# Layer 0's down projection by seven block products a chunk instead of two full products

## The chip, the cores and the metric

The kernel runs on one core of one Trainium2 chip. The metric is the device time of one execution, in microseconds (us). All data is 32-bit floating point.

## The reference, cut to what matters

The reference is a small two-layer network. Each layer normalizes its input and adds an attention part and a feed-forward part to it. The change lies in layer 0's feed-forward part, for 2,048 tokens of width 512 and an inner width of 1,408:

```
xn  = layernorm(x)
g   = (xn @ gate_w.T) * gate_s          # 512 -> 1408
u   = (xn @ up_w.T) * up_s              # 512 -> 1408
out = ((silu(g) * u) @ down_w.T) * down_s   # 1408 -> 512: "the way down"
x   = x + attention0(xn) + out
```

Layer 0's attention is a recurrence: 32 minibatches of 16 tokens (of each of 4 sequences) follow each other, and each one updates a small state matrix that the next one needs. Layer 1, an attention with softmax and a feed-forward part of four experts, comes after layer 0 and is not touched.

## The kernel before, in words

Layer 0 works on 8 chunks of 256 tokens (4 sequences x 64 positions). TensorE (PE) multiplies 128x128 stationary blocks with moving operands of up to 512 columns and adds up in PSUM.

**Fill work.** For each chunk the generator `between(ch)` yields pieces of PE work in order. First come 11 steps `gate_up(ch, i)`: each fetches two weight tiles of 256 KB (`wg`, `wu`, two buffers each) on SP's DMA queue (L471), makes 8 products of 256 columns, and leaves 128 of the 1,408 inner rows in `hid` (L478, on DVE, after an activation on ACT). In chunk 0 `finish_constants` follows (spread of the output scale `dsc` to all partitions, the bias row `brow`). Then `down(ch, u)` runs for the two halves u of the chunk's tokens, mixed with the next chunk's keys, values and queries (`nxt`) and with the end of the previous chunk (`fin`). `down` makes 11 products of 512 columns with tiles `wd` of 256 KB, which SP fetches for each u anew into four buffers (L489). Then DVE multiplies the PSUM result by `dsc` (L494), and GpSimd (POOL) adds `brow` to the rows of x (L495) and that to the result (L496).

**The recurrence.** The main loop takes the 32 minibatches: `prepare(n)` on POOL (load of `kv`, L307, and the tiles `sk`, `km` and the queries in `wq_bd`), `weights_out`, `first_product` (the PE group `pz`), `queries_out` (the PE group `pso`), `gradient` (about 17 DVE instructions), `out_operands` (`gh` on POOL, L421), `update` (PE group `wacc`) and `emit_out`. Between these steps it calls `fill(us)`, which takes pieces from the fill work until their stated costs (the numbers that the pieces yield) cover the given time. The next minibatch's first product needs the state `wacc` that this one has updated.

**Order.** Each engine works through its instructions in the built order, and so does SP with the DMAs it issues: one that waits holds those behind it. A scheduler in the tile framework may place instructions otherwise than the program does; `tc.keep_in_program_order` pins one. A tile of a pool waits for the readers of the tile that had its buffer before.

**Early constants.** At the start POOL's queue fetches small tiles (`sel8`, `tok8`, `ch8`, the row `dsc`) into the pool `one`, whose tiles live through the whole of layer 0.

Of the kernel before, what the change touches and what calls it, by code (L numbers as in the profile page):

```python
# [18 lines left out]
P = 128  # L19
# [13 lines left out]
NS = 8  # L33
# [22 lines left out]
def trunk_kernel(ctx: ExitStack, tc: tile.TileContext, a: dict, out: bass.AP):  # L56
# [49 lines left out]
    with ExitStack() as px:  # L106
# [9 lines left out]
        def mm(out, lhsT, rhs, start=True, stop=True):  # L116
            nc.tensor.matmul(out, lhsT=lhsT, rhs=rhs, start=start, stop=stop, skip_group_check=True)  # L117
# [64 lines left out]
        nc.scalar.dma_start(out=rows_small[:, P:], in_=a["tok"].unsqueeze(0))  # L182
        bones = load(one, "bones", [P, P], eng=nc.scalar)
        m2 = load(one, "m2", [P, 2], eng=nc.scalar)
        gamma_row = wk.tile([P, HS], F32, tag="xr", name="gamma_row")
        gbeta_row = one.tile([P, HS], F32, tag="gbeta_row", name="gbeta_row")
        lrw = load(one, "lrw", [P, NC, P], a["lrw"].rearrange("(c p) m -> p c m", p=P))
        wq_w = load(one, "wq", [P, NC, HS], a["wq"].rearrange("(c p) o -> p c o", p=P))
# [12 lines left out]
        tok = lrb[:, P:]  # L201


        sel8 = one.tile([NS, P], F32, tag="sel8", name="sel8")
        tok8 = one.tile([NS, 2, 4, HD], F32, tag="tok8", name="tok8")
        for h in range(2):
            r = slice(4 * h, 4 * h + 4)
            nc.gpsimd.dma_start(
# [249 lines left out]

        gs = load(one, "gs", [P, NI], eng=nc.gpsimd)
        us = load(one, "us", [P, NI], eng=nc.gpsimd)  # L460
        dsc = one.tile([P, HS], F32, tag="dsc", name="dsc")
        nc.gpsimd.dma_start(out=row["dsc"], in_=a["dsc"].unsqueeze(0))
        hid, yf = {}, {}

# [15 lines left out]
            )  # L480
            yield 3.43

        def down(ch, u):
            xr = wk.tile([P, HS], F32, tag="xr", name=f"xr_{ch}_{u}")
            load_rows(xr, a["x"], ch, u)
            pd = ps_dn.tile([P, HS], F32, tag="pd", name=f"pd_{ch}_{u}")
            for i in range(NI):
                w = wk.tile([P, HS], F32, tag="wd", name=f"wd_{ch}_{u}_{i}", bufs=4)
                nc.sync.dma_start(out=w, in_=a["wd"][i * P : (i + 1) * P, :])  # L489
                mm(pd, hid[ch][:, i, u * P : (u + 1) * P], w, i == 0, i == NI - 1)  # L490
                if i in (3, 7):
                    yield 3.43
            t = wk.tile([P, HS], F32, tag="yf", name=f"yf_{ch}_{u}", bufs=4)
            nc.vector.tensor_mul(t, pd, dsc)  # L494
            nc.gpsimd.tensor_add(xr, xr, brow)  # L495
            nc.gpsimd.tensor_add(t, t, xr)  # L496
            yf[ch, u] = t
            yield 2.57


        ch8 = one.tile([NS, 4, 32], F32, tag="ch8", name="ch8")
        for j, name in enumerate(("gamma", "beta")):
            nc.gpsimd.dma_start(
                out=ch8[4 * j : 4 * j + 4], in_=by_head(name).rearrange("al be h d -> be al (h d)")
# [9 lines left out]

        def finish_constants():
            nc.sync.dma_start(out=wo, in_=a["wo"].rearrange("(c p) o -> p c o", p=P))
            spread_row(dsc, row["dsc"])
            pt = psum()[:, :NS]
            nc.tensor.transpose(pt, ch8.rearrange("s al x -> s (al x)"), ident[:NS, :NS])
            nc.vector.tensor_copy(by_ch, pt)  # L520
            yield 1.0

            pt = psum()[:, :NC]
            mm(pt, onesd, beta_ch)
            beta_m = wk.tile([P, 1], F32, tag="beta_m", name="beta_m", bufs=1)
            nc.vector.tensor_reduce(beta_m, pt, AX.X, ALU.add)
            nc.vector.tensor_scalar(beta_ch, beta_ch, beta_m, None, ALU.subtract)

            pr = psum()
            for c in range(NC):  # L530
                pnb_b = wk.tile([P, P], F32, tag="pnb_b", name=f"pnb_b{c}")
                nc.vector.tensor_copy(pnb_b, pnb[:, c : c + 1].to_broadcast([P, P]))
                mm(pr, pnb_b, wo[:, c, :], c == 0, c == NC - 1)
            nc.vector.tensor_copy(brow, pr)
            for c in range(NC):
                nc.vector.tensor_scalar_mul(wo[:, c, :], wo[:, c, :], pnw[:, c : c + 1])
            yield 3.43
# [118 lines left out]
        def between(ch):  # L656

            fin = finish(ch - 1) if ch > 0 else iter(())
            if ch + 1 == NCHUNK:
                latent_operands()  # L660
            for i in range(NI):
                yield from gate_up(ch, i)
                if ch + 1 == NCHUNK and i in (2, 5, 8):
                    latent_rows(i // 3)
                if i == NI - 3:
                    yield from take(fin, 1)
            if ch == 0:
                yield from finish_constants()
            nxt = iter(())
            if ch + 1 < NCHUNK:  # L670
                nxt = chain(
                    norm_turn(ch + 1), keys(ch + 1), token_tile(ch + 1, 0), token_tile(ch + 1, 1), queries(ch + 1)
                )
            else:
                yield from fin
            for u in range(2):
                dn = down(ch, u)
                for j in range(3):
                    yield from take(nxt, 2)
                    yield from take(dn, 1)  # L680
                    yield from take(fin, 1)
            yield from nxt
            done.add(ch + 1)
            yield from fin
            if ch + 2 < NCHUNK:
                norm_rows(ch + 2)
            if ch + 1 == NCHUNK:
                for key in sorted(parts, key=str):
                    yield from latents(key)
# [842 lines left out]
```

## Time and profile before

| | |
|---|---|
| median of 3 runs | 2003.97 us (2002.03 to 2005.3) |
| the profiled execution's own time | 2001.78 us |
| its span, first to last instruction | 2000.0 us |
| granted TensorE clock, mean | 0.995 |
| PE, DVE, ACT, POOL busy, share of the span | 97%, 59%, 41%, 26% |
| layer 0's end in the trace | near 970 us |
| down products (`pd`, L117) | 166.3 us busy, 352 records of 592 to 697 ns |
| DMA | 273.50 MB, 137 GB/s on average |

The profile comes from one execution. PE's busy time holds the pipelined ends of products, so the pitch from one group's start to the next group's start is the better price of a product. Idle time of an engine that nobody waits for costs nothing.

### The profile page before, as it was taken

What the parts mean: (1) busy time and instruction counts of PE and PEld (TensorE: products, weight loads), DVE (VectorE), ACT (ScalarE), POOL (GpSimd) and SP (SyncE); (2) the same over time, 40 slices, a digit from 0 to 9 for tenths busy, and PEclk for the clock granted to TensorE, in tenths of its full rate; (3) what the DMA queues carried; (4) which work ended last, traced back from release to release, by engine and by line L of the source; (5) the groups of instructions that cost most, each with busy time, mean ns of one, the idle gap of its engine ahead of it and who ended that gap; (6) DMA issues with size and microseconds to landing.
All of it is one profiled execution on the core that took longest, in us unless ns stands there. A gap on an engine that the chain in (4) does not pass through costs nothing.

```text
span 2000.0 us, 32373 instructions
## 1 busy us (share of the span) xinstructions
PE 1939.4 (97%) x11626; PEld 1233.0 (62%) x11626; DVE 1170.9 (59%) x2579; ACT 815.8 (41%) x1695; POOL 515.9 (26%) x619
## 2 busy tenths in 40 slices
PE   8999999999999999998999999999999999999997
PEld 6777676767767676743777745555555555555555
DVE  5445757475666566574555566555655556555664
ACT  2224334334334342432222165554554455445552
POOL 4334343424243343412000101111211121322110
PEclk9999999999999999999999999999999999999999
DMA  6657566646465455746652144444444434333343
GB/s 167 199 138 212 143 188 169 181 115 192 123 172 167 124 175 152 229 117 200 224 167 63 44 112 127 123 102 109 105 103 107 106 102 112 93 97 97 102 107 103
DMA packets 227307, 273.50 MB, mean 137 GB/s; under 512 B 88587, under 2 KB 117452, under 8 KB 226508
## 3 DMA queue, kind: packets, MB, share of 16 engines
q1 hardware_dynamic: 206656, 239.28, 43.5%
q0 software_dynamic: 8992, 26.84, 4.7%
q10 hardware_dynamic: 11500, 5.32, 0.9%
q8 instruction: 93, 1.52, 0.3%
q14 instruction: 66, 0.54, 0.1%
HBM read 174.18 MB, written 34.87 MB: 105 GB/s over the span
## 4 chain that ended last, share of the span: by engine, by line
PE 49%; DVE 1%; DMA 1%; SPq 0%; ACT 0%; issue 0%; DVEq 0%; ACTq 0%
PE pc L1254 11%; PE sc L1207 9%; PE pq L1184 8%; PE px L1301 5%; PE p L1301 4%; PE pk L1184 3%; PE epg L976 3%; PE epo L1039 1%; PE epu L976 1%; PE eox L1069 1%; PE pvo L891 1%; PE pw L866 1%; PE eo L1069 1%; DMA gu<-in_gu 0%; SPq L1246 0%
## 5 line engine op out<-in xcount | busy, mean ns | idle before, releaser
L1225 DVE TENSOR_REDUCE st<-sc 128x1 f32<-128x512 f32 x256 | 168.9, 681 | 242.4 <-PE sc L1207 242.4
L1227 ACT ACTIVATE prob<-sc,st 128x512 f32<-128x512 f32 x256 | 175.1, 686 | 213.7 <-DVE st L1225 213.5
L1254 PE MATMUL pc<-prT,lv 128*128 128x512 f32 x512 | 232.5, 597 | 5.2 <-DMA out<-y 3.9
L1236 DVE STREAM_TRANSPOSE tt<-prob 128x512 f32<-128x512 f32 x256 | 178.4, 700 | 46.6 <-ACT prob L1232 37.1
L1232 ACT ACTIVATE prob<-prob,st 128x512 f32<-128x512 f32 x256 | 182.0, 720 | 58.2 <-DVE st L1231 58.2
L117 PE MATMUL pf<-xT,wg 128*128 128x256 f32 x704 | 174.7, 390 | 4.1 <-DMA wg<-in_wg 2.7
L1184 PE MATMUL pq<-cq,uq 128*128 128x512 f32 x384 | 175.2, 592 | 0.0
L117 PE MATMUL pf<-xT,wu 128*128 128x256 f32 x704 | 168.2, 382 | 0.9 <-DMA wu<-in_wu 0.7
L117 PE MATMUL pd<-wd,hid 128*128 128x512 f32 x352 | 166.3, 601 | 1.3 <-DMA wd<-in_wd 1.3
L1254 PEld LDWEIGHTS pc<-prT,lv 128*128 128x128 f32 x512 | 96.8, 191 | 106.8 <-issue 104.5
L117 PEld LDWEIGHTS pf<-xT,wg 128*128 128x128 f32 x704 | 133.1, 193 | 31.2 <-issue 4.9
L1207 PE MATMUL sc<-k,q 32*128 32x512 f32 x1024 | 145.7, 617 | 2.5 <-ACT prob L1227 2.5
L117 PEld LDWEIGHTS pf<-xT,wu 128*128 128x128 f32 x704 | 134.7, 192 | 20.7 <-DMA wu<-in_wu 2.1
L478 DVE SCALAR_TENSOR_TENSOR hid<-pf,us,sg 128x256 f32<-128x256 f32 x88 | 42.0, 478 | 155.3 <-ACT sg L477 154.9
L1184 PEld LDWEIGHTS pq<-cq,uq 128*128 128x128 f32 x384 | 74.1, 193 | 90.7 <-issue 89.7
L314 POOL TENSOR_SCALAR sk<-k,m 128x256 f32<-128x256 f32 x64 | 60.3, 952 | 180.9 <-PE pz L117 168.7
L1195 POOL TENSOR_TENSOR kr<-kr,t2k 128x512 f32<-128x512 f32 x16 | 20.3, 1268 | 332.3 <-DVE t2k L1194 332.3
L421 POOL TENSOR_SCALAR gh<-grad,m 128x256 f32<-128x256 f32 x64 | 61.9, 976 | 153.2 <-DVE grad L390 131.0
L117 PEld LDWEIGHTS pd<-wd,hid 128*128 128x128 f32 x352 | 63.3, 190 | 60.4 <-issue 44.2
L1207 PEld LDWEIGHTS sc<-k,q 32*128 32x128 f32 x1024 | 48.4, 185 | 82.8 <-issue 73.2
L477 ACT ACTIVATE sg<-pf,gs 128x256 f32<-128x256 f32 x88 | 41.6, 473 | 134.8 <-PE pf L117 134.5
L1256 ACT COPY ctxT<-pc 128x512 f32<-128x512 f32 x64 | 37.4, 584 | 132.0 <-PE pc L1254 132.0
(316 smaller groups left out, 3455.2 us busy)
## 6 DMA issues: line engine op xcount, KB each, us to landing
prT<-tt SPq DMA_DIRECT2D x1016, 64.0 KB, 2.0
wd<-in_wd SPq DMA_DIRECT2D x176, 256.0 KB, 3.1
wg<-in_wg SPq DMA_DIRECT2D x88, 256.0 KB, 3.1
wu<-in_wu SPq DMA_DIRECT2D x88, 256.0 KB, 3.0
cq<-lat_d SPq DMA_DIRECT2D x48, 256.0 KB, 3.8
rows<-rows SPq DMA_DIRECT2D x128, 66.0 KB, 2.2
kv<-rows POOLq DMA_DIRECT2D x32, 264.0 KB, 4.3
gu<-in_gu SPq DMA_DIRECT2D x3, 2048.0 KB
```

The source lines that it names most:

```text
L117: nc.tensor.matmul(out, lhsT=lhsT, rhs=rhs, start=start, stop=stop, skip_group_check=True)
L314: nc.gpsimd.tensor_scalar_mul(sk[:, :, :, h, :], at(k1[ch], slice(0, P)), m2[:, h : h + 1])
L421: nc.gpsimd.tensor_scalar_mul(gh[:, :, h, :], g, m2[:, h : h + 1])
L976: nc.tensor.matmul(ps, lhsT=w[:, c, :], rhs=x[:, c], start=start and c == 0, stop=c == 1, skip_group_check=True)
L1184: nc.tensor.matmul(ps, lhsT=columns(ws[hg][w]), rhs=x, start=(i == 0), stop=(i == len(srcs) - 1))
L1207: nc.tensor.matmul(ps[h], lhsT=qk[f"q{c}"][r, i * P : (i + 1) * P], rhs=qk[f"k{c}"][r, :], start=(n == 0), stop=(n == 2),)
L1225: pin(nc.vector.tensor_reduce(mx, ps[h], AX.X, ALU.max, negate=True))
L1227: pin(nc.scalar.activation(pr, ps[h], AF.Exp, bias=mx, scale=1.0, accum_out=sm))
L1232: pin(nc.scalar.mul(pr, pr, sm))
L1236: nc.vector.transpose(out=tt[:, :, h - 2], in_=pr.rearrange("p (k kq j) -> p kq k j", kq=4, j=32))
L1254: pin(nc.tensor.matmul(pc, lhsT=lv[:, b, k, :], rhs=at[:, :, k, :], start=(k == 0), stop=(k == E - 1)))
L1301: nc.tensor.matmul(ps[:, q, :], lhsT=a[:, k, q * P : (q + 1) * P], rhs=w[:, k, :], start=start and k == 0 and q == 0, stop=k == 1, skip_gr ...
```

## The change

It replaces the two full down products of a chunk by a block scheme. The first ten of the eleven inner row blocks are cut into halves k (5 blocks each), the outputs into halves of 256 columns, and the tokens into the halves u. The eight block products of that 2x2x2 cut become seven, each between a sum of left blocks (from `hid`) and a sum of right blocks (from the weights); each result is added to one to three output quarters. The eleventh row block (`last_d`) is multiplied directly, by four products of 256 columns.

- `down_operands` builds the right operands once, in steps taken during chunk 0's `gate_up` calls: it multiplies the weights by `dsc` on DVE, makes four differences of each block on GpSimd, and stores seven operands of 640 KB in DRAM (`rights_d`).
- `left_sums` makes three sums of 128x640 on DVE in each chunk, two of them into a new tile `hs`; a fourth follows in `down`.
- `down(ch)` loads the operands whole (tile `wd`, now 640 KB, two buffers), makes the seven products of 5 x 256 columns, and adds each PSUM result on DVE to `yf`, which `residual` has filled with the rows of x.
- GpSimd adds `brow` to `yf` once for each u, pinned.
- `gamma_row` moves to the tag `wg`, `sel8`, `tok8` and `ch8` to the tag `gh`, `pnb_b` to the tag `sg`; the tag `xr` is gone. `dsc` becomes a tile of the tag `yf`; `last_d` takes its place in `one`.

```diff
+        KH, half = NI // 2, HS // 2
+        rights_d = dram.tile([7, P, KH, half], F32, tag="rights_d", name="rights_d")
+        def down_operands():
+            dsc = wk.tile([P, HS], F32, tag="yf", name="dsc", bufs=4)
+            spread_row(dsc, row["dsc"])
+            pt = psum()[:, :NS]
+            nc.tensor.transpose(pt, ch8.rearrange("s al x -> s (al x)"), ident[:NS, :NS])
+            nc.vector.tensor_copy(by_ch, pt)
+            nc.sync.dma_start(out=last_d, in_=a["wd"][2 * KH * P :, :])
+            nc.gpsimd.tensor_mul(last_d, last_d, dsc)
+            pairs = a["wd"][: 2 * KH * P].rearrange("(k i p) o -> i p k o", k=2, i=KH)
+            for i in range(KH):
+                raw = wk.tile([P, 2, HS], F32, tag=("hs", "zch")[i % 2], name=f"wd_{i}", bufs=1)
+                nc.sync.dma_start(out=raw, in_=pairs[i])
+                nc.vector.tensor_mul(raw, raw, dsc.unsqueeze(1).to_broadcast([P, 2, HS]))
+                b11, b12, b21, b22 = (raw[:, k, o : o + half] for k in range(2) for o in (0, half))
+                t = wk.tile([P, KH, half], F32, tag="wd", name=f"td_{i}")
+                nc.gpsimd.tensor_sub(t[:, 0], b12, b11)
+                nc.gpsimd.tensor_sub(t[:, 1], b22, t[:, 0])
+                nc.gpsimd.tensor_sub(t[:, 2], b22, b12)
+                nc.gpsimd.tensor_sub(t[:, 3], b21, t[:, 1])
+                nc.sync.dma_start(out=rights_d[0][:, i], in_=b11)
+                nc.sync.dma_start(out=rights_d[1:3, :, i].rearrange("j p o -> p j o"), in_=raw[:, 1].rearrange("p (j o) -> p j o", j=2))
+                nc.sync.dma_start(out=rights_d[3:, :, i].rearrange("j p o -> p j o"), in_=t[:, :4])
+                yield
+        def residual(ch):
+            for u in range(2):
+                t = yf[ch, u] = wk.tile([P, HS], F32, tag="yf", name=f"yf_{ch}_{u}", bufs=4)
+                load_rows(t, a["x"], ch, u)
+        def left_sums(ch):
...
+            s = wk.tile([P, 2, KH, P], F32, tag="hs", name=f"hs_{ch}", bufs=1)
+            nc.vector.tensor_add(s[:, 0], a21, a22)
+            nc.vector.tensor_sub(s[:, 1], s[:, 0], a11)
+            nc.vector.tensor_sub(a21, a11, a21)
-        def down(ch, u):
...
-                w = wk.tile([P, HS], F32, tag="wd", name=f"wd_{ch}_{u}_{i}", bufs=4)
-                nc.sync.dma_start(out=w, in_=a["wd"][i * P : (i + 1) * P, :])
-                mm(pd, hid[ch][:, i, u * P : (u + 1) * P], w, i == 0, i == NI - 1)
...
-            nc.vector.tensor_mul(t, pd, dsc)
-            nc.gpsimd.tensor_add(xr, xr, brow)
-            nc.gpsimd.tensor_add(t, t, xr)
+        def down(ch):
+            def add(ps, u, oh):
+                t = yf[ch, u][:, oh * half : (oh + 1) * half]
+                nc.vector.tensor_add(t, ps, t)
+            def product(ps, x, j, start, more=None):
+                w = wk.tile([P, KH, half], F32, tag="wd", name=f"wd_{ch}_{j}")
+                nc.sync.dma_start(out=w, in_=rights_d[j])
+                for k in range(KH):
+                    mm(ps, x[:, k, :], w[:, k, :], start and k == 0, k == KH - 1 and more is None)
+                if more:
+                    last(ps, *more, False)
...
+            product(x, o["a11"], 0, True)
+            for u in range(2):
+                tc.keep_in_program_order(nc.gpsimd.tensor_add(yf[ch, u], yf[ch, u], brow))
+            add(x, 0, 0)
+            yield 2.16
+            p2 = bank("p2")
+            product(p2[:, 0], o["a12"], 1, True, (0, 0))
+            last(p2[:, 1], 1, 1, True)
...
+            product(x, o["s2"], 4, False)
...
+            nc.vector.tensor_sub(o["a12"], o["a12"], o["s2"])
...
+            product(p5, o["s1"], 3, True)
...
+            product(x, o["a21"], 5, False)
...
+            product(p3, o["a12"], 2, True, (0, 1))
...
+            product(x, o["a22"], 6, False, (1, 0))
@@ between(ch), after each gate_up(ch, i)
+                if ch == 0 and 0 < i <= KH + 1:
+                    next(rights, None)
+                if i == 1:
+                    residual(ch)
+                if i == NI - 2:
+                    left_sums(ch)
...
-            for u in range(2):
-                dn = down(ch, u)
-                for j in range(3):
+            dn = down(ch)
+            for j in range(7):
                     yield from take(nxt, 2)
                     yield from take(dn, 1)
                     yield from take(fin, 1)
```

## The prediction

> **What bounds the kernel now.** I read the page's busy times first, then busy time by stage, then the timelines of PE, POOL and SP where the change starts, 40 to 96 us.
>
> ```profile
> PE 1939.4 (97%) x11626; PEld 1233.0 (62%) x11626; DVE 1170.9 (59%) x2579; ACT 815.8 (41%) x1695; POOL 515.9 (26%) x619
> ```
>
> By stage (us from:to, length; then busy us of PE, PEld, DVE, ACT, POOL; granted clock, DMA share, GB/s):
>
> ```profile
> 47.30:96.00 48.70, 45.35 (x359) 35.97 (x359) 21.26 (x53) 12.26 (x23) 14.88 (x20) 0.93 0.72 208
> 96.00:905.00 809.00, 781.71 (x6589) 558.16 (x6588) 500.86 (x1178) 305.39 (x585) 299.60 (x394) 1.00 0.58 161
> ```
>
> PE is 97% busy, and between 96 and 905 us (most of layer 0) it idles 809.0 - 781.7 = 27 us in all. So work taken from PE there shortens the kernel, and every pause added on PE lengthens it. DVE (62% busy there), POOL and DMA have room on average; they matter where PE stands still for them.
>
> ```profile
> 96.42 3.60 PE L117 MATMUL pd<-wd,hid 128*128 128x512 f32 x8
> 99.86 3.62 PE L117 MATMUL pj<-xT,wk 128*128 128x256 f32 x16
> 103.31 3.60 PE L117 MATMUL pd<-wd,hid 128*128 128x512 f32 x8
> ```
>
> The trace shows two records per product. Four products of 512 columns go from 96.42 to 99.86: 0.86 us each. Eight of 256 columns go from 99.86 to 103.31: 0.431 us each, so halving a product's width halves its price.
>
> **1. The products on PE.** Removed per chunk: 2 x 11 of 512 columns, 22 x 0.86 = 18.9 us. Added: 7 x 5 plus 4 for the eleventh row block, 39 x 0.431 = 16.8. Saved: 2.1 us a chunk, **16.9 us** over 8 chunks. This is certain work off the bound engine.
>
> **2. Chunk 0: building the right operands.** This runs once, but inside the queues that feed PE. Now, from the timelines of PE, POOL and SP (start, length, engine, line, operation; in brackets the idle time before):
>
> ```profile
> 52.84 0.59 PE L117 MATMUL pj<-by_ch,onesd 128*128 128x4 f32 x2 [2.39 <-DVE by_ch L520]
> 53.29 3.76 PE L117 MATMUL pf<-xT,wg 128*128 128x256 f32 x8
> 56.85 2.78 PE L117 MATMUL pf<-xT,wu 128*128 128x256 f32 x8
> 59.47 1.89 PE L117 MATMUL pf<-xT,wg 128*128 128x256 f32 x8
> ```
> ```profile
> 50.91 1.70 POOL L316 COPY wq_bd<-q 32x256 f32<-32x256 f32 x4
> 52.56 1.14 POOL L307 DMA_DIRECT2D kv<-rows  x2
> ...
> 61.14 1.82 POOL L421 TENSOR_SCALAR gh<-grad,m 128x256 f32<-128x256 f32 x2
> ```
> ```profile
> 41.05 0.35 SPq L471 DMA_DIRECT2D wg<-in_wg  x1
> 44.08 0.35 SPq L471 DMA_DIRECT2D wu<-in_wu  x1
> ```
>
> SP fetches gate block 2 at 41 us, PE starts it at 53.3, and gate blocks then follow each other every 3.45 us while minibatch 0's gradient runs beside them. The order in which the built program's instructions stand on each engine differs in three places. (a) On SP the fetch for gate block 2 stands behind the store of the first four sums, and each later fetch behind the store of one more step. (b) On POOL the loads of kv stand behind the scaling of last_d and four subtractions. (c) On PE gate block 2 stands behind minibatch 0's whole update and minibatch 1's first product.
>
> First pause. PE ends gate block 1 at 47.3; the moved spread of dsc and the transpose (1.3), pz (1.5) and its query product (0.6) end at 50.7. dsc is copied on DVE by 49.3. POOL then has last_d (128x512, 1.3), sk (1.8), four subtractions and the copies into wq_bd (1.7). No row shows a 128x256 TENSOR_TENSOR on POOL; 128x512 takes 1.27, so half (0.64) bounds it below and the strided 128x256 TENSOR_SCALAR (0.95) above. I take 0.68, near the half, since it is the same operation: 2.7 for four. kv is issued at 49.3 + 1.3 + 1.8 + 2.7 + 1.7 = 56.8. Now it takes 61.14 - 52.56 = 8.6 from kv to gh: gh starts at 65.4 and ends at 67.2. Then wacc, output product, copies to wq_bd and minibatch 1's first product, 3 us: gate block 2 starts near 70.2 instead of 53.3. Of these 16.9 us, 2.9 is PE work that is now done later. Lost: **14.0 us**.
>
> Then rounds. Steps 1 to 4 each run in a ring: load of 512 KB, product with dsc on DVE, four subtractions on POOL, issue of the stores, and only then SP comes to the next gate block and the next load. A load of 512 KB took 4.0 to 5.5 us (W_DQ, zb), 256 KB 3.1; DVE 128x1024 is 1.21 (zb+q), subtractions 2.7, issues 0.6. I take 3.5 for the load, in the emptier queue of a stalled PE: 8.0 us a round; 7.6 to 11 by the bounds. Step 1's product with dsc stands in minibatch 1's gradient, some 6.3 us after its pz (on DVE now 96.1 to 102.3), at 76.5; its sums are stored at 80.4, and after 5 us of issues and landing block 4 starts at 85.3; then 93.3, 101.3, 108.5 for block 7. From block 2 to block 7 that is 38.3 us. Now it is 73.3 - 53.3 = 20.0; 4.1 of the difference is recurrence work on PE that is now done later. Lost: **14.2 us**.
>
> A pause costs more than its length: after the 2.4 us wait above, the matmuls at 53.29 and 56.85 took 3.76 and 2.78 instead of 1.89, 2.8 us lost. The new pauses (16, 4, 3, 4, 2 us) are mostly followed by another pause that swallows this; I add 1 us net.
>
> The Trainium skill ("TensorE: Matmul & The Clock Gate", Part 1) says the array drops to half clock after about 3.4 us of idling, in a free-running window. The stretch 53.3 to 57 shows a granted clock of 0.50 after 2.4 us, so here shorter pauses also did it. By the page's threshold only three of the new pauses would count, by the row all five; the sum changes by under 1 us.
>
> Term 2 is 14.0 + 14.2 + 1 = **29 us**; by the bounds, 25 (subtractions 0.64, rounds 7.6) to 42 (0.95, rounds 11).
>
> The skill speaks against this part: "GPSIMD Engine Reference", section 4.1, sends two-input elementwise work to VectorE, as GpSimd is about two times slower. By the rows 128x512 takes 1.27 on POOL, 0.69 on DVE. With all subtractions on DVE (0.42 each) a round would be 1.0 shorter and term 2 some 5 us less.
>
> **3. Loads of the right operands.** A product needs a whole 640 KB block, with two buffers; its load starts when the product two before it ends. By the order on PE, the work between the two, priced as above, is 3.0 to 5.2 us ahead of each chunk's third product in chunks 1 to 7, 5.0 to 5.2 ahead of the fourth in three chunks, 4 ahead of the last two in chunk 7, otherwise 6 to 24. Between 512 KB (4.0 to 5.5) and 1 MB (5.7 and more), 640 KB takes 4.5 to 6.4; I take 5.0. The deficits add to 1.5 + 2.0 + 3.7 (chunks 2, 5, 7): **6 us**, 4 to 18 by the bounds. Now PE waits 1.3 us for wd. In bytes the loads shrink, 22 x 256 KB to 7 x 640 KB a chunk, so only their timing costs.
>
> **4. DVE.** Added per chunk: four sums of 128x640 (between 0.69 and 1.21: 0.82 each) and nine additions of 128x256 at 0.42; removed: two of 0.69. That is +5.7 us a chunk, 46 in all, to 68% of the stage, hidden behind PE except where a gradient waits behind a sum. PE's waits for g_bd are 5.3 us now. Below: POOL loses 16 additions of 1.3, and PE's waits for gh (5.8) could go, so -5. Above: one block of three sums in a gradient in each chunk, 8 x 2.5 = 20. I take **+2**, nearer to the row of today's waits, since the order places the sums where gate products run on PE.
>
> Moved at no cost: x's rows come earlier into yf, past SP's gate fetches, 2.4 us of issues in chunk 0, inside the first pause; without that cover they delay gate block 2 by as much. The GpSimd additions of the bias row are pinned behind gh, hence a late one would hold prepare's sk, but x and brow are there long before. The small tiles that moved share buffers whose readers are done. The loads of the next stage wait for the end of chunk 7's down products, as before.
>
> **Sum.** Profiled execution 2001.8 (span 2000.0 plus 1.8): 2001.8 - 16.9 + 29 + 6 + 2 = 2021.9. The median, 2003.97, lies 2.2 above it: **2024 us**.
>
> **The rivals.** *Faster: the lead of the recurrence is paid back.* When gate block 10 ends, minibatches 1 and 2 are already under way; now only minibatch 0 is. If PE's 27 us of waits between 96 and 905 go with it: 2024 - 27 - 6 (the loads hidden too) = 1991. It decides from 24 us given back. Against it: minibatch 4 needs chunk 1's keys, and in the new order its pz again stands behind gate block 7 of chunk 1 (now 6), so the lead is spent. *Larger loss: the rounds are DMA-bound.* DMA is 72% busy at 47 to 96 us, and 11 x 256 KB read and 7 x 640 KB written are added there: term 2 at 42, loads at 16: 2024 + 13 + 10 = 2047. *No change:* stores do not hold SP long and rounds take 4.9: four rounds lose 12 less, term 3 is at its low end of 4, term 4 at -2: 2024 - 12 - 2 - 4 = 2006.
>
> **Chances.** Forecast 0.68, larger loss 0.12, no change 0.07, faster 0.13. What a measurement can tell from no change is 0.2%, 4 us. Faster 0.13, same 0.07, slower 0.80. The range reaches from the no-change case, 2002, to near the larger loss, 2045.
>
> **What would show it.** Right: PE idles some 15 us before gate block 2, which starts near 70; waits for wg of 3 to 4 us before blocks 4, 5 and 6; block 10 ends near 122 instead of 89; down products take 0.431 each; PE waits on wd of several us at third products. Wrong: gate block 2 before 60, rounds near 5 us, or PE idle in 96 to 905 falling well below 27.

## The result and the profile after

The changed kernel takes 2069.99 us (median of 4 runs, 2067.86 to 2075.65), the kernel before 2004.63 us beside it. The ratio is 1.0326, with a 95% interval of 1.0307 to 1.0346: 65 us slower. The forecast was slower too, but 2024 us, with a range of 2002 to 2045. The direction was right, the size 46 us too small.

Profile after (span 2073.9 us, own time 2075.65): first the page's busy times, then the two stages shown of before, with the same columns.

```profile
PE 1946.3 (94%) x11898; PEld 1296.9 (63%) x11898; DVE 1212.6 (58%) x2672; ACT 820.4 (40%) x1697; POOL 513.8 (25%) x624
```
```profile
47.30:96.00 48.70, 22.85 (x251) 17.33 (x250) 27.22 (x56) 10.18 (x21) 30.30 (x37) 0.69 0.45 138
96.00:905.00 809.00, 751.75 (x6443) 602.91 (x6445) 486.96 (x1152) 294.61 (x554) 265.28 (x359) 0.98 0.55 157
```

Where the build runs, PE is busy for 22.9 of 48.7 us (before 45.4), at a granted clock of 0.69 (before 0.93), and the DMA engines are *less* busy, 0.45 for 0.72. But PE also idles 57 us between 96 and 905 us, for 27 before. The predicted pauses are only the first half of the loss.

The first pause, on PE and on POOL (start, length, engine, line, operation, in brackets the idle time before and what ended it):

```profile
71.70 0.32 PE L117 MATMUL pso<-a_bd,gh 128*32 128x68 f32 x1 [19.80 <-POOL gh L422]
...
76.30 1.99 PE L117 MATMUL pf<-xT,wg 128*128 128x256 f32 x8
...
91.76 3.78 PE L117 MATMUL pf<-xT,wg 128*128 128x256 f32 x8 [1.82 <-DMA wg<-in_wg]
```
```profile
50.36 2.24 POOL L495 TENSOR_TENSOR last_d<-last_d,dsc 128x512 f32<-128x512 f32 x1 [8.07 <-issue]
...
54.39 0.71 POOL L503 TENSOR_TENSOR td<-wd 128x256 f32<-128x256 f32 x1
...
59.15 1.15 POOL L308 DMA_DIRECT2D kv<-rows  x2
64.41 2.06 POOL L322 TENSOR_SCALAR km<-kv,m2n 128x256 f32<-128x256 f32 x2 [4.12 <-DMA kv<-rows]
...
69.82 1.83 POOL L422 TENSOR_SCALAR gh<-grad,m 128x256 f32<-128x256 f32 x2
```

kv is issued at 59.2 (forecast 56.8), gh starts at 69.8 (65.4), gate block 2 at 76.3 (70.2). A subtraction takes 0.71 (0.68 taken). Then the rounds, on SP's queue:

```profile
86.02 0.37 SPq L511 DMA_DIRECT2D rights_d<-td  x1
86.45 0.50 SPq L499 DMA_DIRECT2D wd<-in_wd  x1
87.04 0.95 SPq L472 DMA_DIRECT2D wg<-in_wg  x1
...
95.39 0.37 SPq L511 DMA_DIRECT2D rights_d<-td  x1
96.22 0.37 SPq L499 DMA_DIRECT2D wd<-in_wd  x1
96.69 0.66 SPq L472 DMA_DIRECT2D wg<-in_wg  x1
```

Each gate fetch (L472) stands behind the store of four differences (L511), as forecast; a round takes 9.7 us instead of 8.0. The load issued at 86.45 reaches DVE's product at 91.17, so 4.7 us for the 3.5 taken. Block 10 ends at 133.9, not near 122.

The rest of the loss lies in the recurrence. Four places of the timeline of PE, in us, for most of the runs told below (layer 0 ends where PE starts the next stage's first products, `epg`):

| kernel | chunk 1's first gate block | chunk 7's first gate block | recurrence's last output ends | layer 0 ends | ratio to before |
|---|---|---|---|---|---|
| before | 142.6 | 804.6 | 902.9 | 970.5 | 1 |
| changed | 176.5 | 858.9 | 975.7 | 1043.0 | 1.0326 |
| no build | 150.1 | 833.3 | 948.6 | 1012.8 | 1.0205 |
| no sums | 176.4 | 846.6 | 962.5 | 1026.7 | 1.0281 |
| pinned | 169.4 | 840.2 | 963.9 | 1032.6 | 1.0282 |
| pinned, no build | 133.9 | 808.1 | 930.0 | 996.1 | 1.0138 |
| gaps 7.5 alone | 173.7 | 867.4 | 971.1 | 1039.2 | 1.0327 |
| no build, pins, gaps | 135.7 | 809.2 | 911.8 | 985.1 | 1.0048 |
| pinned, from before | 137.5 | 804.4 | 901.7 | 970.8 | 1.0008 |
| ten products, from before | 143.4 | 801.6 | 902.2 | 971.2 | 0.9986 |
| gates and wo on ACT, pins, gaps | 143.3 | 819.0 | 920.3 | 991.0 | 1.0113 |
| the same, sums on POOL | 143.4 | 808.3 | 911.2 | 983.0 | 1.0071 |
| the same, gaps 13, 1, 7.5 | 141.7 | 806.7 | 909.0 | 983.0 | 1.0029 |
| no build, no sums, pins, gaps | 133.4 | 796.6 | 894.7 | 967.7 | 0.9985 |

The changed kernel is 33.9 us behind when chunk 0 is done, 54.3 at chunk 7, 72.8 at the recurrence's end. From there to the end of layer 0 all these kernels need 64 to 74 us. So most of what delays layer 0 delays the recurrence, and the experiments ask what makes that late. The table is read from the profiled executions, which took 2001.78 and 2075.65 us for the kernel before and the changed one: 73.9 us apart, where the medians are 65 apart.

The whole of layer 0 from 47.3 us on, before and changed, with the same columns:

```profile
47.30:970.48 923.18, 885.20 (x7118) 625.76 (x7118) 548.66 (x1290) 332.35 (x653) 325.26 (x431) 0.99 0.59 165
```
```profile
47.30:1043.04 995.74, 891.43 (x7395) 690.12 (x7394) 591.25 (x1385) 336.59 (x655) 323.19 (x436) 0.96 0.53 151
```

Layer 0 ends 72.6 us later. PE waits 104.3 us instead of 38.0, which is 66.3 of them. The other 6.2 are busy time, though the products ask for 16.9 less. The granted clock is 0.96 instead of 0.99, so about 23 us (6.2 + 16.9, an estimate) went into products that ran slower behind the pauses. What PE waited for in the changed kernel between 40 and 1045 us (total, times, longest):

```profile
PE pso L117 <- POOL gh L422: 31.5, 5, 19.8
...
PE wacc L117 <- ACT g_bd L396: 10.5, 3, 5.8
PE pf L117 <- DMA wg<-in_wg: 9.6, 4, 3.9
PE p L117 <- DMA wd<-rights_d: 5.6, 3, 4.3
```

### The profile page after: what moved, and what is told of

The parts are those of the page before. It is cut to its first block, busy times and chain, and to the rows that moved or that the text cites. A ratio compares the mean times of both kernels' runs of the same rounds, so it can differ in the third digit from the quotient of the medians.

```text
span 2073.9 us, 32857 instructions
## 1 busy us (share of the span) xinstructions
PE 1946.3 (94%) x11898; PEld 1296.9 (63%) x11898; DVE 1212.6 (58%) x2672; ACT 820.4 (40%) x1697; POOL 513.8 (25%) x624
## 4 chain that ended last, share of the span: by engine, by line
PE 78%; DVE 8%; DMA 5%; POOL 3%; issue 3%; ACT 2%; SPq 1%; ACTq 0%; DVEq 0%; POOLq 0%
PE pj L117 14%; PE pc L1337 11%; PE pf L117 9%; PE sc L1290 9%; PE pq L1267 8%; PE px L1384 5%; PE p L1384 4%; PE epg L1059 3%; PE pk L1267 3%; PE pd L117 2%; PE p L117 2%; PE pz L117 1%; PE epu L1059 1%; PE epo L1122 1%; PE pso L117 1%
## 5 line engine op out<-in xcount | busy, mean ns | idle before, releaser
L1315 ACT ACTIVATE prob<-prob,st 128x512 f32<-128x512 f32 x256 | 182.0, 721 | 59.2 <-DVE st L1314 59.2
L479 DVE SCALAR_TENSOR_TENSOR hid<-pf,us,sg 128x256 f32<-128x256 f32 x88 | 41.7, 477 | 142.6 <-ACT sg L478 141.9
L322 POOL TENSOR_SCALAR km<-kv,m2n 128x256 f32<-128x256 f32 x64 | 61.3, 965 | 70.6 <-PE wacc L117 42.4
L1357 POOL TENSOR_TENSOR t_ops<-vo 128x512 f32<-128x512 f32 x4 | 5.2, 1293 | 284.5 <-PE eo L1152 199.1
```

The source lines that it names most:

```text
L322: nc.gpsimd.tensor_scalar_mul(km[:, :, :, h, :], kv[:, :, 0:64].rearrange("p b (al d) -> p b al d", d=HD), m2n[:, h : h + 1])
L1315: pin(nc.scalar.mul(pr, pr, sm))
```

## The experiments

All runs were timed beside the kernel before on the same chip. Microseconds of gain below are differences of ratios times 2004. "The whole computation" in an expectation means that nothing is left out.

### One part at a time

**No build.** `down_operands` ends after its first step; `product` loads 640 KB blocks of another array:

```diff
-            pairs = a["wd"][: 2 * KH * P].rearrange("(k i p) o -> i p k o", k=2, i=KH)
-            for i in range(KH):
-                raw = wk.tile([P, 2, HS], F32, tag=("hs", "zch")[i % 2], name=f"wd_{i}", bufs=1)
-                nc.sync.dma_start(out=raw, in_=pairs[i])
...
-                nc.sync.dma_start(out=rights_d[3:, :, i].rearrange("j p o -> p j o"), in_=t[:, :4])
-                yield
+            yield
...
-                nc.sync.dma_start(out=w, in_=rights_d[j])
+                nc.sync.dma_start(out=w, in_=rights_g[j].rearrange("p (k o) -> p k o", k=KH))
```

> Left out: the loop that builds the right operands (loads, product with dsc, subtractions, stores); the seven loads of 640 KB a chunk read blocks of the same size of another array, so the way down has its products, loads and sums. Theory A (chunk 0 pays twice only: its build costs about 36 us, the rest, some 30 us, is lost later in the recurrence, in an order of work that is fixed): about 2070 - 38 = 2032 us, gate block 2 starts before 62 us, and minibatch 29's gradient in chunk 7 is still some 17 us long. Rival B (the later losses follow from the disturbed start): everything but the loads' 6 us goes, about 1995 us, below the kernel before.

Measured: 2044.17 us, ratio 1.0205 (1.0190 to 1.0221), 24 us less than the changed kernel, so nearer to A; B is out. But A missed in two numbers. Gate block 2 starts at 66.7 us, since PE still waits 13.8 us with the loop of the build gone. And 41 us of loss stay instead of some 28. The third sign held: minibatch 29's gradient is still 17 us long.

```profile
64.69 0.32 PE L117 MATMUL pso<-a_bd,gh 128*32 128x68 f32 x1 [13.77 <-POOL gh L422]
```

That wait is one of order: on PE the output product of minibatch 0 stands ahead of gate block 2. The gate products could have run, as the pinned kernel without a build shows below (chunk 0 done 16 us earlier).

**No sums.**

```diff
-            s = wk.tile([P, 2, KH, P], F32, tag="hs", name=f"hs_{ch}", bufs=1)
-            nc.vector.tensor_add(s[:, 0], a21, a22)
-            nc.vector.tensor_sub(s[:, 1], s[:, 0], a11)
-            nc.vector.tensor_sub(a21, a11, a21)
-            left[ch] = dict(a11=a11, a12=a12, a21=a21, a22=a22, s1=s[:, 0], s2=s[:, 1])
+            left[ch] = dict(a11=a11, a12=a12, a21=a21, a22=a22, s1=a21, s2=a22)
...
-            nc.vector.tensor_sub(o["a12"], o["a12"], o["s2"])
```

> Left out: the four sums of left operands in each chunk on VectorE (128x640 each); the products take blocks of hid in their place, with the same matmuls and loads. Theory A (the sums stand inside the gradients, above all in chunk 7, where the end of the recurrence sets the end of the layer): 10 to 20 us less than the changed kernel, about 2055 us, and chunk 7's minibatch 29 takes under 12 us from pz to gradient. Rival C (the order on TensorE alone, with too little work between a gradient and its use, costs it): 3 us less or none, about 2067.

Measured: 2058.56, ratio 1.0281 (1.0264 to 1.0298), 9 us less. The gain is near A's low end, but A's reason does not hold. Minibatch 29 still takes 21.1 us from pz to its update (22.1 in the changed kernel). What fills its gradient is seen on DVE of the changed kernel:

```profile
906.10 0.42 DVE L357 TENSOR_REDUCE s<-pz 128x16 f32<-128x256 f32 x1
...
909.31 1.75 DVE L636 RECIPROCAL pn_rs<-pn_rs 128x256 f32<-128x256 f32 x1
...
913.30 0.77 DVE L527 TENSOR_TENSOR hs<-hid 128x640 f32<-128x640 f32 x1
...
914.53 1.19 DVE L640 TENSOR_TENSOR zb<-zb,q 128x1024 f32<-128x1024 f32 x1
...
922.71 0.42 DVE L391 TENSOR_TENSOR grad<-u,rl 128x256 f32<-128x256 f32 x1
```

The gradient lasts 17.0 us, 906.1 to 923.1, because the reciprocals of the previous chunk's end, its product with q and the sums stand among its instructions. Before, minibatch 29's lasts 9.1 (836.0 to 845.1), with the reciprocals behind it. Without the sums it still lasts 15.5. Over all 32 minibatches the time from the end of pz to the end of the gradient adds up to 322 us before, 328 in the changed kernel and 328 without the sums. So longer gradients are not what the sums cost.

The gain comes in chunks 5 and 6, whose gate blocks are 10.7 us less apart. There PE waits 15.1 us in the changed kernel and 8.4 without the sums, at a granted clock of 0.98 and 1.00; a wait of 4.3 us for `wd` in chunk 5 is gone. By what path the sums bring these waits about stays open.

**Stores on GpSimd's queue; subtractions on VectorE.** Two kernels; the diffs show the first of three stores and the first of four subtractions, the others are changed alike. The second kernel's edit also moves sixteen subtractions of the same form in layer 1 to VectorE.

```diff
-                nc.sync.dma_start(out=rights_d[0][:, i], in_=b11)
+                nc.gpsimd.dma_start(out=rights_d[0][:, i], in_=b11)
```
```diff
-                nc.gpsimd.tensor_sub(t[:, 0], b12, b11)
+                nc.vector.tensor_sub(t[:, 0], b12, b11)
```

> The whole computation; the three stores of each building step are issued on GpSimd's queue instead of SyncE's. Theory D (SyncE's queue, in which each gate fetch waits behind a store that waits for the subtractions, makes the rounds of 10 us): rounds fall to 5 us or less, 15 to 25 us less, about 2050. Rival E (the rounds are bound by the 512 KB loads and by the subtractions themselves): within 8 us of 2070.

> The whole computation; the four subtractions of each building step run on VectorE instead of GpSimd. Theory F (the subtractions' time on GpSimd is in each round and ahead of the first loads of kv): rounds 1 us shorter, first pause 3 us shorter, 5 to 8 us less, about 2063. Rival G (VectorE's gradients of minibatches 0 and 1 pay what GpSimd saves): 2070 or more.

Measured: 2060.28, ratio 1.0285 (1.0269 to 1.0300), 8 us less, and 2057.89, ratio 1.0274 (1.0259 to 1.0289), 10 us less. The first lies at the edge of rival E: chunk 1's first gate block comes 12.6 us earlier (163.9), of which a third is lost again by the end. Its rounds do not fall to 5 us as D said: loads are issued at 81.5 and 91.9 us. The second is F's answer, a little more than F said, with a first pause of 16.0 us (19.8) and rounds of 9.2 and 7.8 us. The subtractions moved in layer 1 have little part in it: from layer 0's end to the end of the kernel it takes 1029.9 us, the changed kernel 1030.8. Neither part alone is the loss.

### The order on PE

**Pins.** The first matmul of pz, of the update and of the output of each minibatch is pinned behind the fill work that the program puts ahead of it. The diff shows pz; the update and the output are treated alike:

```diff
-            mm(pz[:, :, :HD], bones, gsum.rearrange("p b al d -> p (b al) d"), True, False)
+            ins = mm(pz[:, :, :HD], bones, gsum.rearrange("p b al d -> p (b al) d"), True, False)
+            if n in PINNED:
+                tc.keep_in_program_order(ins)
```

> The whole computation of the changed kernel; in each minibatch the first matmul of pz, of the update (wacc) and of the output (pso<-a_bd) is pinned behind the PE work that the program puts ahead of it, so that 9 us or more of products stand between pz and the first use of the gradient (as the changed kernel is ordered: 0.3, 6.5, 2.8 and 3.7 us for minibatches 0, 1, 3 and 7). Theory H (much of the loss is this order: PE stands still for a gradient with nothing to do): the waits for gh and g_bd fall from some 44 us to under 15, and the kernel takes 25 us less, about 2045 us. Rival I (the building steps hold PE as long in another place, since each gate fetch still waits on SyncE behind a store): waits for wg grow by what the waits for gh lose, 2060 us or more.

Measured: 2061.84, ratio 1.0282 (1.0259 to 1.0304), 9 us less. The time is rival I's. The waits for gh and g_bd fell from 44.5 to 12.4 us, as H said, and PE stood still in another place, for the gate fetches behind the build, though these waits grew by 14.5 us (9.6 to 24.1) and not by all of the 32 that the others lost:

```profile
61.95 3.65 PE L118 MATMUL pf<-xT,wg 128*128 128x256 f32 x8 [13.48 <-DMA wg<-in_wg]
```
```profile
PE pf L118 <- DMA wg<-in_wg: 24.1, 5, 13.5
```

> As the pinned kernel, and the three stores of each building step are issued on GpSimd's queue. By theories H and D together (order on PE, and gate fetches behind stores): both losses go, about 2020 us. If the stores on GpSimd's queue hold kv, gh and wq_bd instead: as the pinned kernel or slower.

Measured: 2050.72, ratio 1.0231 (1.0214 to 1.0249). The gain of 19 us is about the sum of the two alone (9 and 8), and 2020 was far off.

> Left out: the loop that builds the right operands (the loads of 640 KB read another array of the same size), as in the first experiment; with the pinned order. If order and build explain the loss together: 2003 - 17 + 6 (loads) + 2 (DVE) = 1994 us, within 8. If 2015 or more, a third cost is left, in the sums on VectorE or in the loads.

Measured: 2033.79, ratio 1.0138 (1.0114 to 1.0161). With build and order both mended, chunk 1's first gate block comes at 133.9 us, 8.7 *earlier* than before, and yet the kernel is 28 us slower than before. A third cost is left, and it lies after chunk 0.

**Control.**

> The kernel before with the same three pins in each minibatch: a control. Its order has 10 us of products or more ahead of each gradient's use already (7.6 once), so by theory H it stays within 6 us of 2003. If it gains 15 us or more, pins help in any order, and what they gain in the changed kernel says little on its loss.

Measured: 2005.71, ratio 1.0008 (0.9994 to 1.0022). Pins do nothing for the kernel before. They do bring chunk 1's first gate block 5 us forward there (137.5), so this mark alone does not tell what a kernel has lost.

### Is the saving worth anything?

**A gap shorter.** I formed a new theory: the planner's gaps pace the recurrence, and the saved products come off the end.

```diff
-GAPS, LAST_GAPS = (11.0, 3.0, 8.0), (10.0, 3.0, 7.0)
+GAPS, LAST_GAPS = (11.0, 3.0, 7.5), (10.0, 3.0, 7.0)
```

> The whole computation of the changed kernel; one number changed: the last of the three gaps of fill work in each of minibatches 0 to 27 is 7.5 instead of 8.0. The kernel's planner hands out 716.8 us of stated fill work before the recurrence ends in the changed kernel and 720.2 in the kernel before, though the whole fill work fell from 754.6 to 737.4; with 7.5 it is 703.0, and 34.4 us are left for the chain after the recurrence, as before. Theory J (the saved products never shorten the kernel, because the gaps fix the recurrence's pace and the saving comes off the end, where PE then waits): about 14 us less, 2056 us, and the stretch from chunk 7's first gate block to the end of layer 0 falls from 184 to some 166 us. Rival K (the end of layer 0 is late through VectorE alone): within 4 us of 2070.

Measured: 2071.39, ratio 1.0327 (1.0309 to 1.0344): nothing. The stretch from chunk 7's first gate block to the end of layer 0 did fall, from 184 to 172 us, but chunk 7 began 8.5 us later. The time is rival K's, but the shorter stretch does not fit K. By itself theory J falls.

> Left out: the loop that builds the right operands (the loads of 640 KB read another array of the same size). With gaps of 7.5 and the pins in minibatches 0 to 4, 7 and 8 alone. If build, order and pace together are the whole loss: the sum's 1994 + 6 of the loads, 1995 to 2005 us. If it stays above 2015, more is lost in the sums and loads than any of these theories says.

Measured: 2015.73, ratio 1.0048 (1.0031 to 1.0065), 18 us less than the pinned kernel without a build. It is just above 2015, so by its own answer something is still lost in the sums and loads. Pins in seven minibatches and shorter gaps help together; which of the two helps more was not tried. The gain lies in chunk 7 alone: its first gate block comes at 809.2 us (808.1 before this step), the recurrence's end at 911.8 (930.0).

> The kernel before with gaps of 7.5: a control. There the recurrence waits for the keys of its next chunk (by the planner's sums 720.2 us of fill work are handed out before its end with 8.0 and with 7.5), so theory J expects no gain: 2000 to 2010 us. If it gains 10 us or more, a smaller gap helps any of these kernels and says nothing on the change.

Measured: 2020.18, ratio 1.0079 (1.0063 to 1.0094): a miss, 16 us slower. Half a microsecond in one gap costs the kernel before about as much as the products can save. So a difference of that size between kernels with other gaps or stated costs can come from the order alone.

**Ten products.** To price the saving without build or sums, the kernel before loses one of its eleven products in each half:

```diff
-            for i in range(NI):
+            for i in range(NI - 1):
...
-                mm(pd, hid[ch][:, i, u * P : (u + 1) * P], w, i == 0, i == NI - 1)
+                mm(pd, hid[ch][:, i, u * P : (u + 1) * P], w, i == 0, i == NI - 2)
```

> The kernel before; left out: the eleventh product of each down product (10 instead of 11 of 512 columns) and its weight load, with the stated costs of the pieces unchanged, so the planner hands out the same pieces. That takes 2 x 0.86 us off PE in each chunk, 13.8 in all, about what the changed kernel saves. By step 1 of the prediction (work off the bound engine shortens the kernel by its own time): 2004 - 14 = 1990 us. If the recurrence sets the pace and PE's saved time turns into waits: 2000 us or more.

> As the kernel before with ten products (the eleventh is left out), and the stated cost of the last piece of each half is lowered by 0.86 as well, as the change lowers its own: the planner then hands out 3.4 us less stated work before the recurrence ends and keeps 14 less for the chain after it. By step 1 alone: 1990 us again. If lowered stated costs shift fill work ahead of the recurrence and starve its end: 5 to 15 us above the run with unchanged costs.

Measured: 2000.60, ratio 0.9986 (0.9970 to 1.0002), and 2005.47, ratio 1.0004 (0.9986 to 1.0021). Of 13.8 us taken from PE, 2.8 came out (0 to 6 by the interval), and none with the stated cost lowered (`yield 1.71` for `yield 2.57`). The recurrence's last output ends at 902.2 us, before at 902.9. The waits show where the time went, first before, then with ten products (47 to 1000 us):

```profile
PE pso L117 <- POOL gh L421: 5.8, 4, 2.7
```
```profile
PE pso L117 <- POOL gh L421: 12.5, 6, 5.6
```

And layer 0 as a whole, with ten products (before it is the line shown with the result):

```profile
47.30:971.20 923.90, 880.25 (x7098) 625.14 (x7097) 550.78 (x1291) 335.51 (x655) 329.43 (x431) 0.98 0.56 161
```

Of the 13.8 us, 5.7 became waits (43.7 us for 38.0), and PE's busy time fell by only 5.0: the other 9 went into products at a lower clock. This is not the profiled execution alone; all ten runs had a granted clock of 0.989 on average, the kernel before beside them 0.993. The order on PE differs in a few pieces as well.

PE was busy for 97% and still its saved work did not shorten the kernel by as much. It had about the work that fills the time in which a gradient runs on DVE; with less, it waits for gh and runs slower behind the waits.

### Mending the queue, and what remains

**Chunk 0's gate fetches on ScalarE's queue**, with the seven pins and the shorter gaps; then the load of wo as well:

```diff
-                nc.sync.dma_start(out=w, in_=a[nm][i])
+                (nc.sync if ch else nc.scalar).dma_start(out=w, in_=a[nm][i])
...
-            nc.sync.dma_start(out=wo, in_=a["wo"].rearrange("(c p) o -> p c o", p=P))
+            nc.scalar.dma_start(out=wo, in_=a["wo"].rearrange("(c p) o -> p c o", p=P))
```

> The whole computation of the changed kernel, with three mends: chunk 0's gate fetches are issued on ScalarE's queue, so that none of them waits on SyncE behind a store or a load of the build; the pins in minibatches 0 to 4, 7 and 8; gaps of 7.5. If gate fetches behind the build's DMAs are what chunk 0 loses: waits for wg before blocks 2 to 10 under 8 us in all, and 2005 to 2015 us. If the fetches then compete with the build for the DMA engines: some 2030 us.

> The whole computation: chunk 0's gate fetches and the load of wo on ScalarE's queue, pins in minibatches 0 to 4, 7 and 8, gaps of 7.5. With wo on SyncE PE stood still for it for 17.4 us at the end of chunk 0. If that wait is all that chunk 0 still loses: about 2018 us and chunk 1's first gate block near 136 us. If the load of wo only moves behind other work: 2030 or more.

Measured: 2035.69, ratio 1.0151 (1.0136 to 1.0166), and 2025.74, ratio 1.0113 (1.0079 to 1.0147). The first has the time of the second answer but not its cause: no block of chunk 0 waits as much as 0.3 us for wg, but wo, still behind the build on SP, held PE for 17.4 us:

```profile
103.19 5.55 PE L118 MATMUL pj<-wo,pnb_b 128*128 128x512 f32 x8 [17.43 <-DMA wo<-in_wo]
```

In the second the same stage looks like that of before, with the whole build in it, here by stage and on PE:

```profile
47.30:96.00 48.70, 43.28 (x313) 33.11 (x311) 26.70 (x51) 10.78 (x21) 31.18 (x39) 0.96 0.79 245
```
```profile
51.56 1.89 PE L118 MATMUL pf<-xT,wg 128*128 128x256 f32 x8
...
55.02 1.89 PE L118 MATMUL pf<-xT,wg 128*128 128x256 f32 x8
```

Gate blocks follow each other every 3.5 us while the DMA engines are busy for 0.79, more than in any kernel here without this mend. So it was not the DMA engines that held the gate blocks back, but the order on one queue. The time is 8 us above its expectation: the build still costs 8 to 9 us at chunk 1's first gate block (143.3, against 133.9 and 135.7 without a build), and 13 us by the ratios (1.0113 against 1.0048 without a build). The kernel before with its fetches on ScalarE's queue was not run, so how much that move gives without any build is open.

**The sums on GpSimd** (the first of four is shown).

> As the kernel with wo on ScalarE's queue, and the four sums of left operands in each chunk run on GpSimd instead of VectorE. By theory C's opposite (the sums hold gradients on VectorE, about 10 us as the run without sums showed): 2005 to 2010 us. If on GpSimd they hold gh and the tiles of prepare as long: 2018 or more.

```diff
-            nc.vector.tensor_add(s[:, 0], a21, a22)
+            nc.gpsimd.tensor_add(s[:, 0], a21, a22)
```

Measured: 2017.90, ratio 1.0071 (1.0048 to 1.0094), 8 us less than with the sums on VectorE. The gain is near what the run without sums showed, the time at the edge of the second answer, since the kernel it starts from was 8 us above its own expectation. The reason given does not hold here either: from the end of pz to the end of the gradient the 32 minibatches take 338 us, with the sums on VectorE 330.

> Left out: the loop that builds the right operands (the loads of 640 KB read another array of the same size) and all four sums of left operands; pins in minibatches 0 to 4, 7 and 8, gaps of 7.5. What is left of the change is its 39 products of 256 columns, its loads and its additions. By step 1 of the prediction: 2003 - 17 + 6 = 1992 us. If PE's saved time turns into waits, as with ten products in the kernel before (2.8 of 13.8 us came out): 2000 to 2008.

Measured: 2003.04, ratio 0.9985 (0.9969 to 1.0000). The products, loads and additions of the change, with everything else taken away, are worth 3 us, at the edge of what the interval tells from nothing. Beside the run with sums (1.0048) this puts the four sums at 13 us. Layer 0 as a whole:

```profile
47.30:967.72 920.42, 869.07 (x7389) 676.04 (x7390) 561.79 (x1348) 339.77 (x658) 307.36 (x416) 0.99 0.54 155
```

PE is busy for 16.1 us less than before, about what the products save, at the same clock, and waits 13.4 us more (51.4 for 38.0). The recurrence ends 8.2 us earlier than before, layer 0 only 2.8: behind the recurrence it needs 73.0 us, before 67.5.

> As the run with gates and wo on ScalarE's queue and the sums on GpSimd, with the gaps 13, 1 and 7.5 (12, 1 and 7 in the last chunk): the same stated fill work in each minibatch, but more of it between pz and the first use of the gradient. If waits for gradients are what is left: 5 to 10 us less than that run, 2008 to 2013. If not: 2015 or more.

```diff
-GAPS, LAST_GAPS = (11.0, 3.0, 7.5), (10.0, 3.0, 7.0)
+GAPS, LAST_GAPS = (13.0, 1.0, 7.5), (12.0, 1.0, 7.0)
```

Measured: 2012.18, ratio 1.0029 (1.0014 to 1.0045): as expected, 8 us less. The reason is not shown: PE's one wait for gh is 5.2 us in both traces, and layer 0 ends at 983.0 us in both. This is the best full version. It recovers 60 of the 65 us and is still not faster than the kernel before.

## Why the prediction was wrong

Two steps failed: the passage from saved PE work to saved time in step 1, and the recurrence's order from chunk 1 on, for which the sum had no term. The build was right in its mechanism and too small.

1. **The products (-16.9): the price was right, the step from it to the time was wrong.** Five products of 256 columns take 2.16 us from start to start (864.29 to 866.45 in the pinned kernel without a build), 0.431 each, as said. But "certain work off the bound engine" failed: 13.8 us taken off gave 2.8, and the change's own products, stripped of the rest, gave 3. I read 97% busy and 27 us of idle time as a bound. The saved time turned into waits and into products at a lower clock, since the recurrence, minibatch by minibatch, and the end behind it go on at their own pace with PE's fill work beside them. This step is off by 14 us.
2. **Chunk 0's build (+29, bounds 25 to 42).** Mechanism right, in all three places named, and the size between the bounds, 7 above the value: the changed kernel is 33.9 behind at chunk 1's first gate block, 36 with the 2.1 that the products give back. 26 us of it go when the build alone is taken out, and 16 more when PE's order is mended as well, of which pins alone bring 5 in the kernel before. The first pause was 19.8 us, not 16 (scaling of last_d 2.24 for 1.3, and the gap from kv to gh 10.7 for 8.6: km, which stands in it both times, starts 5.3 us after the issue of kv, 3.2 before), the rounds 9.7, not 8.0 (the load 4.7 for 3.5).
3. **Half clock (+1): too small.** By PE's busy time it is about 23 us in layer 0 (the estimate given with the result). About 5 of these lie ahead of 200 us; the rest follows later pauses, which the sum did not have. The row used in the prediction shows half clock after a wait of 2.4 us, so it does not speak for the shortest of the five pauses, 2 us.
4. **Loads (+6): right in size, in part by luck.** PE waits 5.6 us for wd, 4.3 of it at chunk 5's third product, where the prediction had 2.0. Chunks 2 and 7, with 1.5 and 3.7, show none above 1 us.
5. **DVE (+2, bounds -5 to +20): the value was wrong, the bound held.** The sums cost 9 us (run without them) to 13 (beside the run without a build). How they do so is open: DVE's own order does put some into gradients, but all gradients together take as long without the sums, 328 us.
6. **Left out altogether: the recurrence's own turn.** From chunk 1 on I compared work with work. In the order on PE only 2.8 us of products stand between pz and update of minibatch 3, and 3.7 before the output of minibatch 7 (counted from the order at the prices above); a gradient needs 8 to 13 in most minibatches. PE waits there 5.8 and 7.4 us. From chunk 1's first gate block to the recurrence's end the changed kernel loses 39 us more (72.8 - 33.9), where my sum had a gain of 7 (-14.7 + 6 + 2). Half of the 39 us come in chunk 7, from its first gate block to the recurrence's end, before and changed:

```profile
804.62:902.95 98.33, 92.65 (x792) 60.54 (x790) 62.70 (x140) 35.53 (x63) 32.82 (x44) 0.98 0.55 170
```
```profile
858.88:975.70 116.82, 105.54 (x922) 74.11 (x920) 71.90 (x166) 37.56 (x75) 35.78 (x49) 0.99 0.44 140
```

PE is busy for 12.9 of these 18.5 us, with 130 more records. The change's own products in a chunk account for 34 of them (two records for each of 39 - 22); the rest is fill work that is handed out ahead of the recurrence's end. With the shorter gaps and seven pins, and no build, the stretch has 826 records, just those 34 more, and takes 102.6 us. In the chunks between, the 20 us are waits. With pins and gaps, and without build and sums, the whole way from chunk 1's first gate block to the recurrence's end is 761 us again (before 760, changed 799); how much each has by itself in the changed kernel depends on the others and stays open, as gaps alone gave nothing.

Of the rivals, "DMA-bound rounds" gave the nearest time, 2047, with a wrong cause: the DMA share fell to 0.45. "Faster" stood on the lead of the recurrence being paid back; it never was, the recurrence fell further behind.

The Trainium skill ("Perfetto Trace Analysis", Identifying the Most-Contended Engine) says to optimise the engine with the highest occupancy first, and warns that matmul busy time is a poor measure of how near PE is to its limit. Here PE had the highest occupancy by far, and relieving it by 13.8 us gave 2.8, so the rule did not find what bounds this kernel. The warning was in place, though the page gives it for another reason, the pipelining of products.

## What to carry to other kernels

An engine that is busy for 97% because it was given just enough filler for a serial chain is not the bound: before counting saved work as saved time, find the chain that ends last and take a little work out of the filler as a test. A one-time preparation costs by what it stands ahead of in a queue; keep its loads and stores, and what the main engine needs next, on different queues. When the work between two steps changes, look at what each engine's order now puts between a result's start and its use.

## What the runs showed of the hardware

The same pause does not always lead to half clock. Before, and in the pinned kernel without a build, PE waits 2.88 us for the same step; the following four records take 1.98 us in one and 3.78 in the other, at a granted clock of 1.00 and 0.50:

```profile
923.20 1.98 PE L117 MATMUL pj<-pn_sq,bones 128*128 128x512 f32 x4 [2.88 <-ACT pn_sq L549]
```
```profile
950.26 3.78 PE L118 MATMUL pj<-pn_sq,bones 128*128 128x512 f32 x4 [2.88 <-ACT pn_sq L620]
```

The Trainium skill ("TensorE: Matmul & The Clock Gate", Part 1) names a free-running window of about 3.4 us. That the window runs freely fits these two rows; that a whole idle window is needed does not, as 2.88 us were enough once.

VectorE and GpSimd slowed each other in the build. GpSimd's scaling of last_d (128x512) took 2.24 us beside VectorE's 1.23 us product with dsc, and 1.28 in the run without a build, where no such product stands beside it:

```profile
49.38 1.28 POOL L497 TENSOR_TENSOR last_d<-last_d,dsc 128x512 f32<-128x512 f32 x1 [8.07 <-issue]
```

That is 1 us of the 3.8 between the first pause forecast and the one measured. VectorE's product `xh<-xh,s` (128x256) took 0.94 us at 84.5, while GpSimd subtracted, and 0.41 to 0.43 in 30 of its 32 turns; with the sums on GpSimd it once took 1.76 us beside one of them (634.1).
